# A graph layer on one core: norm split in two, gate ahead of it, three more picks, and smaller moves in setup and tail

## The chip, the cores and the metric

The kernel runs on one core of a Trainium2 chip. Its engines are TensorE (PE; its weight loads are listed as PEld), VectorE (DVE), ScalarE (ACT), GpSimd (POOL) and SyncE (SP), which only issues DMAs. The metric is the device time of one execution in microseconds; the time before is the median of three runs. Every engine works through its own queue in the order of the program; the program's order is written out by hand here (`tc.manual_schedule()`), so where a line stands decides when its engine comes to it.

## What is computed

200,000 edges, sorted by destination, between 6,250 nodes of 64 features:

```python
w = silu(edge_attr @ W1 + b1) @ W2 + b2                          # (E, 9)
msg = einsum('ef,em,fmg->eg', x[src], edge_sh * w, W_tp)         # (E, 64)
agg = segment_sum(msg, dst, N) / sqrt(AVG_DEG)                   # AVG_DEG = 16
gamma, beta = split(silu(node_vec[:, None] @ Wn1 + bn1) @ Wn2 + bn2)
out = layernorm(x + agg * (1 + gamma) + beta)                    # each row of 64
```

## The kernel before

**Tiles.** 128 edges make a tile, 16 tiles a block; there are 1,563 tiles and 98 blocks, the last one of 11 tiles. Nodes are in 49 blocks of 128.

**Rows of x.** A tile's 128 source rows come in one of three ways. Most tiles are gathered from HBM by POOL, one indirect DMA per tile (`gather`, L99), six blocks ahead (`AHEAD`); nothing else is on POOL's queue in the main loop. In 23 blocks (`SPG`, every fourth from 7) the first tile comes as 128 single-row DMAs from SP (`load_rows`, L115), 32 of them in each of four iterations. And the last three or four tiles of each block are *picked* out of SBUF by TensorE: `hots` (L521, VectorE) makes one-hot matrices from the tile's keys, `pick` (L536) multiplies them with x in 14 matmuls of 448 columns, one for each of seven column groups and for the high and the low part of x, and VectorE masks and reduces the result (`xm` L545, `hs` L547). `picked(g)` says how many tiles of block g are picked: four, and three where g is divisible by six, which makes 375 picks and 1,165 gathers.

**Keys.** A key tells in which partition and column of x in SBUF a source row lies. Keys are worked out on VectorE for many blocks at once, turned by TensorE (`keys_turn`, L177), copied by ScalarE to `kt` and stored by SP to a table `kd` in HBM (L179), from which `load_keys` (L453) broadcasts them two blocks at a time. Three such tables are stored: one in setup, one each for iterations 3 and 5, whose stores wait in the list `stores` until the next iteration begins.

**One iteration i** of the main loop works on several blocks. It first issues `gather(i + 6)`, then SP's work: whatever is in `stores`; on even i `load(i + 2)`, the edge attributes `ea` (L433, 512 KB for two blocks) and `sh` (L435); on odd i `load_keys`; then `load_rows`. TensorE's order is:

- pick 0 of block i+1, with the matmuls of `nodes(i)` between its own;
- `hidden(i + 2)` (L465), which needs `ea`, and on ScalarE its Silu (L474);
- `second(i + 1)` (L483), which needs PSUM bank "s";
- `windows(i)` (L569), which needs all rows of block i;
- on odd i `project` (L616), with W_tp, for two blocks;
- picks 1, 2 and 3 of block i+1. `weights(i + 1)` on VectorE goes with pick 1.

**Nodes.** `nodes(i)` holds one bank "s" tile `ps`. Into it go the product for the gate of node block i-2 (L661), the placing of sums by node (`place`, L632), and, in every fourth iteration from 7 to 95, the finished sums of two node blocks (`bring`, L648). `gate` (L405, L406) reads its product from `ps` into `gam` and `xb`; it runs for 49 node blocks, up to iteration 50. `bring` calls `finish`, and this `finish_nodes`, the norm: on VectorE `y` = sums x gam (L770), + xb (L771), mean (L773, L774), subtract (L775), square (L777), sum (L779); Sqrt on ScalarE (L782); reciprocal (L783) and the output `o` (L785) on VectorE. All of it stands in VectorE's queue where `bring` is, ahead of the gate. The store of `o` (L418) goes into `stores`.

**Banks.** PSUM tiles are by tag: "px" and "pz" with two buffers, "p1" (two banks: hidden layer, and the transposed projection `pt`), "s" and "r" with one. The keys of a block, `pk` (L515), are in "r", and so is the projection `pr` (L610) of the first block, which has no partner.

**Setup** splits x into a high part (`xs[0]`, L277, ScalarE) and a rest (`xs[1]`, L278, VectorE), in seven pieces; it reads x in order and writes with a stride of seven elements, the layout that the picks need.

**Tail.** After the last pick come the matmuls of the last two node blocks into one tile `py_n` (L739, L743), the windows of block 97, its projection `pr_n` (L751) in 10 matmuls, its placing (L754), and one norm over both node blocks.

Of the kernel before, what the change touches and what calls it, by code (L numbers as in the profile page):

```python
# [7 lines left out]
F32 = mybir.dt.float32  # L8
# [16 lines left out]
KW = KB * W  # L25
ZT = 8
FB = 2
AHEAD = 6
LB = 2
# [21 lines left out]

def picked(g):

    return Q - (g % 6 == 0)


def tiles(g):
# [10 lines left out]
def gnn_resnorm_kernel(ctx: ExitStack, tc: tile.TileContext, x, src, dst, dst_row, ea, sh, cn,  # L68
# [18 lines left out]
    with ExitStack() as fast:  # L87
# [85 lines left out]
        def keys_turn(g0, kf, tag, kt):  # L173

            c0 = g0 * Q
            p_kt = psum.tile([P, P], F32, tag=tag, name=f"p_kt{g0}", bufs=1 + (tag == "pz"))
            nc.tensor.transpose(p_kt, kf, ident)  # L177
            nc.scalar.copy(kt, p_kt)
            stores.append(lambda: nc.sync.dma_start(kd[c0:c0 + P, :], kt))  # L179

        def relative(k0, k1):
            nc.vector.tensor_sub(rel[:, k0:k1], dst_i[:, k0:k1], row_r[:, k0:k1])
# [9 lines left out]
        def setup(temp):  # L192
# [79 lines left out]
                return spread  # L272

            def split(h):
                xh = gam[:, h * J:(h + 1) * J, :]
                hi, lo_ = [xs[i][:, h].rearrange("p f l -> p l f") for i in range(2)]
                nc.scalar.copy(hi, xh)  # L277
                nc.vector.tensor_sub(lo_, xh, hi.bitcast(F32))  # L278

            kb = [ztw[:, k * LB * Q:(k + 1) * LB * Q] for k in range(6)]  # L280
            for f in keys_of(0, LB, kb):
# [29 lines left out]
            pick(0, 2)  # L311
            hidden(1, act=False)
            kt = temp.tile([P, P], F16)
            keys_turn(LB, kb[0], "pz", kt)
            hidden_act(1)
            while stores:
                stores.pop(0)()
            load_keys(LB)
            p_row = psum.tile([len(SPG), P], F32, tag="pz", name="p_row", bufs=2)
            nc.tensor.transpose(p_row, row_f, ident)  # L320
# [88 lines left out]

        stores = []  # L410

        def finish(j0, j1, sums, parts=None):
            y = late.tile([P, j1 - j0, F], F32, tag="y", name=f"y{j0}")
            end = finish_nodes(nc, late, eps, sums, y, gam[:, j0:j1, :], xb[:, j0:j1, :], j0)

            def store():
                o = end()
                stores.append(lambda: nc.sync.dma_start(out_v[:, j0:j1, :], o))  # L418

            if parts is None:  # L420
                store()
            else:
                parts.append(store)


        ea_t, sh_t, oh_t, kr_t, st, a, zs = {}, {}, {}, {}, {}, {}, {}
# [175 lines left out]
        def project(q):  # L602


            gs = pair(q)
            z = [zs.pop(g).rearrange("p c k w -> p c (k w)") for g in gs]
            if len(gs) == 1:
                pr = psum.tile([P, 1, F], F32, tag="r", name=f"pr{q}")
                for c in range(5):
                    nc.tensor.matmul(pr[0:KW, 0], z[0][:, c], wtc2[:, c, :], start=(c == 0), stop=(c == 4))  # L610
                halves(q, pr[0:KW])
# [12 lines left out]

            return [lambda: None, lambda: None, turn]
# [16 lines left out]

            return [lambda k=k: part(k) for k in range(len(gs))]

        def bring(j0, j1, py, ends=None):

            def part(j):
                nc.tensor.matmul(py[:, j - j0], yt.pop(j), ident2, start=True, stop=True)  # L648
                if j == j1 - 1:
                    finish(j0, j1, py[:, 0:j1 - j0], ends)  # L650

            return [lambda j=j: part(j) for j in range(j0, j1)]

        def nodes(i):


            ps = psum.tile([P, 4, P], F32, tag="s", name=f"ps{i}")
            parts = []
            if 0 <= i - 2 < NJ:
                def product(j=i - 2):  # L660
                    nc.tensor.matmul(ps[:, 2], ht[j // 4 % 2][:, j % 4], wn2a, start=True, stop=True)  # L661
                parts.append(product)
            if i % 2 == 0 and i >= 2:
                parts += place(i // 2 - 1, ps[:, 0:2].rearrange("p a n -> p (a n)"))
            j = (i - 5) // 2
            if i % 2 == 1 and i >= 5 and j % FB == FB - 1:
                parts += bring(j + 1 - FB, j + 1, ps[:, 3].rearrange("p (j f) -> p j f", f=F))
            if 0 <= i - 2 < NJ:
                parts.append(lambda: gate(i - 2, ps[:, 2]))
            if i == 60:  # L670
                parts.append(lambda: reach_all(ps[0:1, 3, 0:4]))
            return parts

        with tc.manual_schedule(), tc.tile_pool(name="temp", bufs=1) as temp:
# [2 lines left out]
                       6: [lambda k=k: relative(KN + k, min(KN + k + 352, NBLK * KB))  # L677
                           for k in range(0, NBLK * KB - KN, 352)]}

            for i in range(1, NBLK):  # L680
                if i + AHEAD < NBLK:
                    gather(i + AHEAD)
# [46 lines left out]
            ends = []  # L729
            for f in bring(q - 2, q - 1, psum.tile([P, 1, F], F32, tag="r", name="py_l"), ends):  # L730
                f()
            windows(g - 1)
            sums(g)
            pick(g, 2, [ends])
            pick(g, 3, [project(q)])
            while stores:
                stores.pop(0)()
            py = psum.tile([P, FB, F], F32, tag="s", name="py_n")
            nc.tensor.matmul(py[:, 0], carry.pop(q - 1), ident2, start=True, stop=False)  # L739
            for b in range(2):  # L740
                for k, h in enumerate(pair(q)):
                    for s in range(2):
                        nc.tensor.matmul(py[:, b], hot[h][:, b * P:(b + 1) * P], r[q][:, k, s],  # L743
                                         start=(b == 1 and k == 0 and s == 0), stop=(b == 0 and k == 1 and s == 1))
# [4 lines left out]
            pr = psum.tile([P, F], F32, tag="r", name="pr_n")  # L749
# [6 lines left out]
            while stores:  # L756
                stores.pop(0)()


    bad_n = nc.values_load(flag_i[0:1, 0:1], min_val=0, max_val=4 * P,  # L760
# [6 lines left out]
def finish_nodes(nc, work, eps, sums, y, gam, xb, tag):  # L767

    n = y.shape[1]
    nc.vector.tensor_mul(y, sums, gam)  # L770
    nc.vector.tensor_add(y, y, xb)  # L771
    mean = work.tile([P, n], F32, tag="mean", name=f"mean{tag}")
    nc.vector.tensor_reduce(mean, y, AX.X, ALU.add)  # L773
    nc.vector.tensor_scalar(mean, mean, 1.0 / F, None, op0=ALU.mult)  # L774
    nc.vector.tensor_sub(y, y, mean.unsqueeze(2).to_broadcast([P, n, F]))  # L775
    sq = work.tile([P, n, F], F32, tag="sq", name=f"sq{tag}")
    nc.vector.tensor_mul(sq, y, y)  # L777
    var = work.tile([P, n], F32, tag="var", name=f"var{tag}")
    nc.vector.tensor_reduce(var, sq, AX.X, ALU.add)  # L779

    def end():
        nc.scalar.activation(var, var, AF.Sqrt, bias=eps, scale=1.0 / F)  # L782
        nc.vector.reciprocal(var, var)  # L783
        o = work.tile([P, n, F], F32, tag="o", name=f"o{tag}")
        nc.vector.tensor_mul(o, y, var.unsqueeze(2).to_broadcast([P, n, F]))  # L785
        return o

    return end


def general_path(tc, dram, x, dst_row, ea, sh, src_i, dst_i, w1bd, b1c, w2bd, b2r, wtc,
# [3 lines left out]
    with ExitStack() as ctx:  # L795
# [109 lines left out]
        for j0 in range(0, NJ, JC):  # L905
# [7 lines left out]
            o = finish_nodes(nc, work, eps, a[0], a[0], gam[:, js, :], xb[:, js, :], f"g{j0}")()  # L913
            nc.sync.dma_start(out_v[:, js, :], o)


# [47 lines left out]
```

## Time and profile before

| | us |
|---|---|
| median of three runs (1487.76 to 1489.39) | 1488.75 |
| profiled execution, its own time | 1488.34 |
| profiled execution, span | 1486.5 |
| PE busy in the span | 1443.6 (97%) |
| DVE busy | 1210.6 (81%) |
| POOL busy | 1108.5 (75%) |
| ACT busy | 515.7 (35%) |

The span runs from the first to the last instruction of the profiled execution. A busy share is an average over stages. In the profile, "L99" is line 99 of the kernel; "out<-in" gives the tiles written and read by the program's names with their numbers left out; "x" is a count. A row of the costliest groups ends with the engine's idle time just before its instructions and with what ended most of it ("issue" means that the profile shows nothing that the engine waited for). A row of the waits has a waiting engine and line, what released it, the total in us, how often, and the longest.

### The profile page before, as it was taken

How to read it: one execution, taken by the hardware profiler on the slowest of the kernel's cores; microseconds unless marked ns; L12 is line 12 of the kernel's file. 1: busy time of each engine (PE TensorE's matmuls, PEld its weight loads, DVE VectorE, ACT ScalarE, POOL GpSimd, SP SyncE). 2: the span in 40 equal slices, each digit the busy share in tenths (PEclk: the TensorE clock that was granted, in tenths of full speed). 3: DMA queues.
4: the chain of work that ended last, by engine and by line, in shares of the span. 5: the costliest groups of instructions: out<-in, count | busy, mean ns of one | idle time of the engine just before them, and what ended most of it. 6: DMA issues, size and time to landing. Idle time of an engine off the chain costs nothing.

```text
span 1486.5 us, 34308 instructions
## 1 busy us (share of the span) xinstructions
PE 1443.6 (97%) x10905; PEld 1211.5 (82%) x10905; DVE 1210.6 (81%) x2188; ACT 515.7 (35%) x1324; POOL 1108.5 (75%) x1174
## 2 busy tenths in 40 slices
PE   7899999999999999999999999999999999999997
PEld 5687888888888888888878888888888888888886
DVE  8788887887878888888797888888887888888875
ACT  4324333242433333424243324233242333333332
POOL 7777777777777777777777777777777777777773
PEclk9999999999999999999999999999999999999998
DMA  6422222222223222222232222222222222232310
GB/s 194 96 50 61 73 60 64 68 63 64 55 57 74 62 61 55 77 56 63 55 72 55 61 65 63 61 56 63 64 62 54 73 55 61 55 74 61 73 29 19
DMA packets 90168, 96.03 MB, mean 65 GB/s; under 512 B 36696, under 2 KB 51242, under 8 KB 89978
## 3 DMA queue, kind: packets, MB, share of 16 engines
q0 software_dynamic: 37280, 38.25, 13.4%
q1 hardware_dynamic: 52122, 53.89, 12.5%
q8 instruction: 89, 1.46, 0.4%
q10 hardware_dynamic: 576, 1.61, 0.3%
q14 instruction: 101, 0.83, 0.2%
HBM read 91.91 MB, written 1.73 MB: 63 GB/s over the span
## 4 chain that ended last, share of the span: by engine, by line
PE 79%; POOL 5%; DVE 5%; issue 4%; DMA 3%; ACT 3%; SPq 2%; ACTq 0%; DVEq 0%; POOLq 0%
PE px L536 60%; PE pz L569 6%; POOL hs L99 5%; PE p L465 5%; PE pt L616 3%; PE p L483 3%; DMA hs<-in_x_dram,src_i 2%; SPq L115 1%; ACT st L474 1%; DVE xm L545 1%; ACT L474 1%; PE ps L632 1%; DVE hs L547 1%; PE ps L661 1%; DVE hot_k L521 0%
## 5 line engine op out<-in xcount | busy, mean ns | idle before, releaser
L99 POOL DMA_INDIRECT hs<-in_x_dram,src_i x1165 | 1107.2, 950 | 357.1 <-issue 321.1
L536 PE MATMUL px<-xs_w,hot_k 128*128 128x448 f32 x5250 | 1125.2, 368 | 1.5 <-DVE hot_k L521 1.4
L536 PEld LDWEIGHTS px<-xs_w,hot_k 128*128 128x128 f32 x5250 | 961.2, 189 | 79.9 <-DVE xm L545 2.3
L545 DVE SCALAR_TENSOR_TENSOR xm<-li,jl,px 128x448 f32<-128x448 f32 x375 | 253.4, 676 | 205.3 <-PE px L536 202.6
L521 DVE TENSOR_TENSOR hot_k<-pk,nk 128x896 fp32r<-128x896 f32 x375 | 390.9, 1081 | 0.6 <-ACT pk L515 0.6
L547 DVE TENSOR_REDUCE hs<-xm 128x64 f32<-128x448 f32 x375 | 232.5, 620 | 12.9
L474 ACT ACTIVATE st<-p,b1c 128x1024 f32<-128x1024 f32 x98 | 109.2, 1114 | 374.8 <-PE p L465 374.5
L580 ACT COPY ztw<-pz 64x140 f32<-64x140 f32 (+1 forms) x780 | 208.6, 267 | 14.1 <-PE pz__24815 L569 3.0
L569 PEld LDWEIGHTS pz<-a,hs 128*64 128x64 f32 x3116 | 99.6, 138 | 44.2 <-issue 39.3
L503 DVE TENSOR_TENSOR a<-oh,p 128x1008 f32<-128x1008 f32 x98 | 117.9, 1204 | 3.3
L638 ACT COPY carry<-ps 128x128 f32<-128x128 f32 x48 | 12.7, 265 | 304.8 <-PE ps L632 304.8
L569 PE MATMUL pz<-a,hs 128*64 128x63 f32 x3116 | 112.8, 225 | 4.4 <-DMA hs<-in_x_dram,src_i 1.6
L465 PE MATMUL p<-ea,w1bd 64*128 64x512 f32 x392 | 110.7, 641 | 2.3 <-DMA ea<-in_ea_dram 2.3
L483 PEld LDWEIGHTS p<-st,w2p 128*32 128x32 f32 x784 | 15.8, 108 | 80.7 <-issue 38.5
L782 ACT ACTIVATE var<-var,eps 128x2 f32<-128x2 f32 (+1 forms) x25 | 7.4, 295 | 202.0 <-DVE var L779 202.0
L483 PE MATMUL p<-st,w2p 128*32 128x256 f32 x784 | 62.6, 391 | 7.6 <-DVE xb L406 7.6
L616 PE MATMUL pt<-ztw,wtc 128*64 128x112 f32 x960 | 55.3, 261 | 3.1 <-ACT st L474 2.5
L515 ACT CAST pk<-kr 128x512 f32<-128x512 f16 (+1 forms) x96 | 54.9, 572 | 7.2 <-issue 7.2
L465 PEld LDWEIGHTS p<-ea,w1bd 64*128 64x128 f32 x392 | 29.6, 185 | 31.5 <-issue 24.4
L497 DVE TENSOR_TENSOR p<-p,sh 128x72 f32<-128x72 f32 x196 | 47.3, 241 | 6.7
L616 PEld LDWEIGHTS pt<-ztw,wtc 128*64 128x64 f32 x960 | 46.8, 137 | 5.0 <-ACT st L474 3.9
L486 ACT ACTIVATE p2s<-p,b2c 128x256 f32<-128x256 f32 x98 | 45.7, 466 | 5.7 <-PE p L483 5.7
(150 smaller groups left out, 503.3 us busy)
## 6 DMA issues: line engine op xcount, KB each, us to landing
hs<-in_x_dram SPq DMA_DIRECT2D x2944, 0.2 KB
ea<-in_ea_dram SPq DMA_DIRECT2D x48, 512.0 KB
hs<-in_x_dram,src_i POOLq DMA_INDIRECT x1165
kr<-kd SPq DMA_DIRECT2D x48, 256.0 KB
sh<-in_sh_dram SPq DMA_DIRECT2D x49, 144.0 KB
cb<-cn_d SPq DMA_DIRECT2D x12, 128.0 KB
out_dram<-o SPq DMA_DIRECT2D x24, 64.0 KB
dst_i<-in_dst_dram SPq DMA_DIRECT2D x1, 768.0 KB
```

The source lines that it names most:

```text
L99: hs_dma[g] = [nc.gpsimd.indirect_dma_start(out=hs[g][:, t - g * KB, :], out_offset=None, in_=x, in_offset=bass.IndirectOffsetOnAxis(ap=sr ...
L465: nc.tensor.matmul(p1[:, i, :].rearrange("p (c t e) -> p c t e", c=4, t=4), w1bd[i * 64:(i + 1) * 64, :], e[i * 64:(i + 1) * 64, :].rearra ...
L474: nc.scalar.activation(st[g], p1_t.pop(g), AF.Silu, bias=b1c)
L483: nc.tensor.matmul(p2[g][c * D:(c + 1) * D, 0, :].rearrange("p (i e) -> p i e", i=2), w2p, s[:, :, c * P:(c + 1) * P], start=True, stop=True)
L503: nc.vector.tensor_mul(a[g], oh_t.pop(g)[:, :, None, :].to_broadcast([P, KB, M, W]), sw.unsqueeze(3).to_broadcast([P, KB, M, W]))
L521: nc.vector.tensor_tensor(hot_k[g, t], pk_t[g][:, t, None, :].to_broadcast([P, J, P]), nk.unsqueeze(2).to_broadcast([P, J, P]), op=ALU.is_ ...
L536: nc.tensor.matmul(px.rearrange("p f l -> p (f l)"), hot_k[g, t][:, h, :], xs[i][:, h].rearrange("p f l -> p (f l)"), start=(h == 0 and i ...
L545: nc.vector.scalar_tensor_tensor(xm, li[:, None, :].to_broadcast([P, F, J]), jl[:, c:c + 1], px, op0=ALU.is_equal, op1=ALU.mult)
L547: nc.vector.tensor_reduce(hs[g][:, tiles(g) - q + t, :], xm, AX.X, ALU.add)
L569: mm = nc.tensor.matmul(pz[v][v * F:(v + 1) * F, k // 2].rearrange("p m w -> p (m w)"), hsg[:, k0 + k, :], ag[:, k0 + k].rearrange("p m w ...
L580: copy(z[h * F:(h + 1) * F, 0:5 - h, k0 + v:k0 + n:2, :].rearrange("p m k w -> p k m w"), pz[v][v * F:(v + 1) * F, 0:(n + 1 - v) // 2, h:M ...
L616: nc.tensor.matmul(pt[h * F:(h + 1) * F, 0, 0:KW], wtc2[:, c, :], z[h][:, c], start=(c == 0), stop=(c == 4))
```

## The change

- `picked`: three picks where g is divisible by seven instead of six, hence 378 picks and 1,162 gathers.
- `nodes`: the gate comes ahead of the norm. `bring` holds its matmuls alone; `finish` follows the gate.
- `finish_nodes` is cut into three: the product with gam at once; a `middle` (from the addition to the Sqrt) that the loop calls after pick 1 of the next block; an `end` (reciprocal, output, and the store put into `stores`) that it calls after pick 2.
- Key tables of iterations 3 and 5: their stores wait in a list of their own, `tables`, which is emptied behind the loads and row copies of the next iteration.
- `project` of group 0 takes tag "p1" instead of "r".
- `split` reads x with the stride and writes in order.
- Tail: the first windows of block 97 go ahead of the matmuls of the last node blocks; these two have a bank each; the last projection goes in two halves of its output rows; each of the two is normed alone by `finish_block`, with the bn_stats and bn_aggr instructions.

```diff
 def picked(g):
-    return Q - (g % 6 == 0)
+    return Q - (g % 7 == 0)
...
             def split(h):
-                xh = gam[:, h * J:(h + 1) * J, :]
-                hi, lo_ = [xs[i][:, h].rearrange("p f l -> p l f") for i in range(2)]
-                nc.scalar.copy(hi, xh)
-                nc.vector.tensor_sub(lo_, xh, hi.bitcast(F32))
+                xh = gam[:, h * J:(h + 1) * J, :].rearrange("p l f -> p f l")
+                nc.scalar.copy(xs[0][:, h], xh)
+                nc.vector.tensor_sub(xs[1][:, h], xh, xs[0][:, h].bitcast(F32))
...
-        def finish(j0, j1, sums, parts=None):
+        def finish(j0, j1, sums):
             y = late.tile([P, j1 - j0, F], F32, tag="y", name=f"y{j0}")
-            end = finish_nodes(nc, late, eps, sums, y, gam[:, j0:j1, :], xb[:, j0:j1, :], j0)
+            middle, end = finish_nodes(nc, late, eps, sums, y, gam[:, j0:j1, :], xb[:, j0:j1, :], j0)
             def store():
                 o = end()
                 stores.append(lambda: nc.sync.dma_start(out_v[:, j0:j1, :], o))
...
+            ends.extend([middle, store])
+
+        def finish_block(j, sums):
+            y = late.tile([P, 1, F], F32, tag="y", name=f"y{j}")[:, 0]
+            nc.vector.tensor_mul(y, sums, gam[:, j])
+            nc.vector.tensor_add(y, y, xb[:, j])
+            st = late.tile([P, 6], F32, tag="sq", name=f"st{j}")
+            nc.vector.bn_stats(st, y)
+            mv = late.tile([P, 2], F32, tag="mean", name=f"mv{j}")
+            nc.vector.bn_aggr(mv, st)
+            var = late.tile([P, 1], F32, tag="var", name=f"var{j}")
+            nc.scalar.activation(var, mv[:, 1:2], AF.Sqrt, bias=eps)
+            def end():
+                nc.vector.reciprocal(var, var)
+                o = late.tile([P, 1, F], F32, tag="o", name=f"o{j}")
+                nc.vector.tensor_scalar(o[:, 0], y, mv[:, 0:1], var, op0=ALU.subtract, op1=ALU.mult)
+                nc.sync.dma_start(out_v[:, j:j + 1, :], o)
+            return end
...
             if len(gs) == 1:
-                pr = psum.tile([P, 1, F], F32, tag="r", name=f"pr{q}")
+                pr = psum.tile([P, 2, 4 * P], F32, tag="p1", name=f"pr{q}")
...
         def nodes(i):
...
+            whole = i % 2 == 1 and i >= 5 and j % FB == FB - 1
+            if whole:
+                parts += bring(j + 1 - FB, j + 1, py)
             if 0 <= i - 2 < NJ:
                 parts.append(lambda: gate(i - 2, ps[:, 2]))
+            if whole:
+                parts.append(lambda: finish(j + 1 - FB, j + 1, py))
...
             for i in range(1, NBLK):
                 if i + AHEAD < NBLK:
                     gather(i + AHEAD)
                 while stores:
                     stores.pop(0)()
...
+                while tables:
+                    tables.pop()()
...
                 pick(i + 1, 1, [weights(i + 1), turn])
+                if ends:
+                    ends.pop(0)()
...
                     if t < Q:
                         pick(i + 1, t)
+                    if t == 2 and ends:
+                        ends.pop(0)()
                 if i in (3, 5):
-                    keys_turn(LB + KC * (i - 1) // 2, kb[0], "s", kt)
+                    tables.append(keys_turn(LB + KC * (i - 1) // 2, kb[0], "s", kt))
...
-            py = psum.tile([P, FB, F], F32, tag="s", name="py_n")
-            nc.tensor.matmul(py[:, 0], carry.pop(q - 1), ident2, start=True, stop=False)
+            windows(g, [0])
+            py = [psum.tile([P, F], F32, tag=tag, name=f"py_{tag}") for tag in ("s", "r")]
+            nc.tensor.matmul(py[0], carry.pop(q - 1), ident2, start=True, stop=False)
...
-            windows(g, [0])
             marks(NJ)
             windows(g, [ZT])
...
             for c in range(5):
-                nc.tensor.matmul(pr[0:KW], z[:, c], wtc2[:, c, :], start=(c == 0), stop=(c == 4))
+                for k0, k1 in ((0, F), (F, KW)):
+                    nc.tensor.matmul(pr[k0:k1, 0, 0:F], z[:, c, k0:k1], wtc2[:, c, :], start=(c == 0), stop=(c == 4))
+            end = finish_block(q - 1, py[0])
             last = work.tile([KW, F], F32, tag="rt", name="last")
-            nc.vector.tensor_copy(last, pr[0:KW])
-            nc.tensor.matmul(py[:, 1], hot[g][:, 0:P].bitcast(F32), last, start=False, stop=True)
-            finish(q - 1, NJ, py)
-            while stores:
-                stores.pop(0)()
+            nc.vector.tensor_copy(last, pr[0:KW, 0, 0:F])
+            end()
+            nc.tensor.matmul(py[1], hot[g][:, 0:P].bitcast(F32), last, start=False, stop=True)
+            finish_block(q, py[1])()
...
 def finish_nodes(nc, work, eps, sums, y, gam, xb, tag):
     n = y.shape[1]
     nc.vector.tensor_mul(y, sums, gam)
-    nc.vector.tensor_add(y, y, xb)
...
+    def middle():
+        nc.vector.tensor_add(y, y, xb)
...
+        nc.vector.tensor_reduce(var, sq, AX.X, ALU.add)
+        nc.scalar.activation(var, var, AF.Sqrt, bias=eps, scale=1.0 / F)
     def end():
-        nc.scalar.activation(var, var, AF.Sqrt, bias=eps, scale=1.0 / F)
         nc.vector.reciprocal(var, var)
         o = work.tile([P, n, F], F32, tag="o", name=f"o{tag}")
         nc.vector.tensor_mul(o, y, var.unsqueeze(2).to_broadcast([P, n, F]))
         return o
-    return end
+    return middle, end
```

More of the change, by code (lines that the diff above doesn't have):

```diff
@@ L178, in keys_turn @@
             nc.scalar.copy(kt, p_kt)
-            stores.append(lambda: nc.sync.dma_start(kd[c0:c0 + P, :], kt))
+            return lambda: nc.sync.dma_start(kd[c0:c0 + P, :], kt)
         def relative(k0, k1):
@@ L313, in setup @@
             kt = temp.tile([P, P], F16)
-            keys_turn(LB, kb[0], "pz", kt)
+            keys_turn(LB, kb[0], "pz", kt)()
             hidden_act(1)
-            while stores:
-                stores.pop(0)()
             load_keys(LB)
@@ L410, in gnn_resnorm_kernel @@
         stores = []
-        def finish(j0, j1, sums, parts=None):
+        ends = []
+        def finish(j0, j1, sums):
             y = late.tile([P, j1 - j0, F], F32, tag="y", name=f"y{j0}")
-            end = finish_nodes(nc, late, eps, sums, y, gam[:, j0:j1, :], xb[:, j0:j1, :], j0)
+            middle, end = finish_nodes(nc, late, eps, sums, y, gam[:, j0:j1, :], xb[:, j0:j1, :], j0)
             def store():
@@ L418, in store @@
                 stores.append(lambda: nc.sync.dma_start(out_v[:, j0:j1, :], o))
[L420 to L423, printed above, removed]
+            ends.extend([middle, store])
[15 more added lines that the diff above has]
+            return end
         ea_t, sh_t, oh_t, kr_t, st, a, zs = {}, {}, {}, {}, {}, {}, {}
@@ L607, in project @@
             if len(gs) == 1:
-                pr = psum.tile([P, 1, F], F32, tag="r", name=f"pr{q}")
+                pr = psum.tile([P, 2, 4 * P], F32, tag="p1", name=f"pr{q}")
                 for c in range(5):
-                    nc.tensor.matmul(pr[0:KW, 0], z[0][:, c], wtc2[:, c, :], start=(c == 0), stop=(c == 4))
-                halves(q, pr[0:KW])
+                    nc.tensor.matmul(pr[0:KW, 0, 0:F], z[0][:, c], wtc2[:, c, :], start=(c == 0), stop=(c == 4))
+                halves(q, pr[0:KW, 0:1, 0:F])
                 return []
@@ L643, in place, with bring @@
             return [lambda k=k: part(k) for k in range(len(gs))]
[L645 to L652, printed above, removed]
+        def bring(j0, j1, py):
+            return [lambda j=j: nc.tensor.matmul(py[:, j - j0], yt.pop(j), ident2, start=True, stop=True)
+                    for j in range(j0, j1)]
         def nodes(i):
@@ L665, in nodes @@
             j = (i - 5) // 2
-            if i % 2 == 1 and i >= 5 and j % FB == FB - 1:
-                parts += bring(j + 1 - FB, j + 1, ps[:, 3].rearrange("p (j f) -> p j f", f=F))
+            py = ps[:, 3].rearrange("p (j f) -> p j f", f=F)
+            whole = i % 2 == 1 and i >= 5 and j % FB == FB - 1
+            if whole:
+                parts += bring(j + 1 - FB, j + 1, py)
             if 0 <= i - 2 < NJ:
                 parts.append(lambda: gate(i - 2, ps[:, 2]))
+            if whole:
+                parts.append(lambda: finish(j + 1 - FB, j + 1, py))
             if i == 60:
@@ L678, in gnn_resnorm_kernel @@
                            for k in range(0, NBLK * KB - KN, 352)]}
+            tables = []
             for i in range(1, NBLK):
@@ L728, in gnn_resnorm_kernel @@
             pick(g, 1, [weights(g)])
-            ends = []
-            for f in bring(q - 2, q - 1, psum.tile([P, 1, F], F32, tag="r", name="py_l"), ends):
-                f()
+            py = psum.tile([P, 1, F], F32, tag="r", name="py_l")
+            for f in bring(q - 2, q - 1, py):
+                f()
+            finish(q - 2, q - 1, py)
+            ends.pop(0)()
             windows(g - 1)
@@ L742, in gnn_resnorm_kernel @@
                     for s in range(2):
-                        nc.tensor.matmul(py[:, b], hot[h][:, b * P:(b + 1) * P], r[q][:, k, s],
+                        nc.tensor.matmul(py[b], hot[h][:, b * P:(b + 1) * P], r[q][:, k, s],
                                          start=(b == 1 and k == 0 and s == 0), stop=(b == 0 and k == 1 and s == 1))
-            windows(g, [0])
             marks(NJ)
@@ L748, in gnn_resnorm_kernel @@
             z = zs.pop(g).rearrange("p c k w -> p c (k w)")
-            pr = psum.tile([P, F], F32, tag="r", name="pr_n")
+            pr = psum.tile([P, 2, 4 * P], F32, tag="p1", name="pr_n")
             for c in range(5):
-                nc.tensor.matmul(pr[0:KW], z[:, c], wtc2[:, c, :], start=(c == 0), stop=(c == 4))
+                for k0, k1 in ((0, F), (F, KW)):
+                    nc.tensor.matmul(pr[k0:k1, 0, 0:F], z[:, c, k0:k1], wtc2[:, c, :], start=(c == 0), stop=(c == 4))
+            end = finish_block(q - 1, py[0])
             last = work.tile([KW, F], F32, tag="rt", name="last")
-            nc.vector.tensor_copy(last, pr[0:KW])
-            nc.tensor.matmul(py[:, 1], hot[g][:, 0:P].bitcast(F32), last, start=False, stop=True)
-            finish(q - 1, NJ, py)
-            while stores:
-                stores.pop(0)()
+            nc.vector.tensor_copy(last, pr[0:KW, 0, 0:F])
+            end()
+            nc.tensor.matmul(py[1], hot[g][:, 0:P].bitcast(F32), last, start=False, stop=True)
+            finish_block(q, py[1])()
     bad_n = nc.values_load(flag_i[0:1, 0:1], min_val=0, max_val=4 * P,
@@ L770, in finish_nodes @@
     nc.vector.tensor_mul(y, sums, gam)
-    nc.vector.tensor_add(y, y, xb)
[L772 to L777, printed above, removed]
-    var = work.tile([P, n], F32, tag="var", name=f"var{tag}")
-    nc.vector.tensor_reduce(var, sq, AX.X, ALU.add)
+    var = work.tile([P, n], F32, tag="var", name=f"var{tag}")
+    def middle():
+        nc.vector.tensor_add(y, y, xb)
+        mean = work.tile([P, n], F32, tag="mean", name=f"mean{tag}")
+        nc.vector.tensor_reduce(mean, y, AX.X, ALU.add)
+        nc.vector.tensor_scalar(mean, mean, 1.0 / F, None, op0=ALU.mult)
+        nc.vector.tensor_sub(y, y, mean.unsqueeze(2).to_broadcast([P, n, F]))
+        sq = work.tile([P, n, F], F32, tag="sq", name=f"sq{tag}")
+        nc.vector.tensor_mul(sq, y, y)
+        nc.vector.tensor_reduce(var, sq, AX.X, ALU.add)
+        nc.scalar.activation(var, var, AF.Sqrt, bias=eps, scale=1.0 / F)
     def end():
-        nc.scalar.activation(var, var, AF.Sqrt, bias=eps, scale=1.0 / F)
         nc.vector.reciprocal(var, var)
@@ L912, in general_path @@
             nc.vector.tensor_add(a[0], a[0], a[2])
-            o = finish_nodes(nc, work, eps, a[0], a[0], gam[:, js, :], xb[:, js, :], f"g{j0}")()
-            nc.sync.dma_start(out_v[:, js, :], o)
+            middle, end = finish_nodes(nc, work, eps, a[0], a[0], gam[:, js, :], xb[:, js, :], f"g{j0}")
+            middle()
+            nc.sync.dma_start(out_v[:, js, :], end())
 _INS = ['x', 'src', 'dst', 'dst_row', 'ea', 'sh', 'cn', 'w1', 'b1', 'w2', 'b2', 'wtp',
```

## The prediction

> **What bounds it now.** I read the page's busy shares, its costliest groups, the waits, a table by stage, then the timelines of one stage.
>
> ```profile
> PE 1443.6 (97%) x10905; PEld 1211.5 (82%) x10905; DVE 1210.6 (81%) x2188; ACT 515.7 (35%) x1324; POOL 1108.5 (75%) x1174
> ...
> L99 POOL DMA_INDIRECT hs<-in_x_dram,src_i x1165 | 1107.2, 950 | 357.1 <-issue 321.1
> L536 PE MATMUL px<-xs_w,hot_k 128*128 128x448 f32 x5250 | 1125.2, 368 | 1.5 <-DVE hot_k L521 1.4
> ```
>
> TensorE is busy 97% of the span, 78% of that in the picks (375 x 14 matmuls). POOL looks freer than it is: its 357 us of idle time is almost all "issue", 0.3 us between gathers, so a gather costs 1.25 us and the 1165 of them run without a break from 4.0 to 1466.2. So there are two streams, and TensorE's is the longer one: the windows matmuls (L569) of the last block start at 1472.07, 5.9 us after its last gather.
>
> The stage table cuts the span at the hidden-layer matmuls (L465) of successive blocks, taken as a block's zero time h:
>
> ```profile
> 667.28:682.09 14.81, 14.81 (x107) 12.59 (x106) 11.78 (x22) 5.28 (x12) 11.32 (x12) 1.00 0.23 55
> 682.09:699.02 16.93, 15.99 (x127) 13.31 (x126) 14.66 (x30) 6.41 (x16) 12.75 (x14) 1.00 0.31 71
> 699.02:713.38 14.36, 14.36 (x104) 12.14 (x103) 12.00 (x20) 3.99 (x11) 10.90 (x12) 1.00 0.25 48
> 713.38:729.06 15.68, 15.68 (x127) 13.32 (x126) 12.08 (x23) 5.33 (x15) 11.83 (x13) 1.00 0.36 89
> ```
>
> Columns: stage, its length, then busy time of PE, PEld, DVE, ACT and POOL. The second and fourth do the same TensorE work (127 matmuls), but the second follows a norm of two node blocks and takes 1.25 us more, with PE idle for 0.94. The waits say whom it waits for:
>
> ```profile
> PE p L483 <- DVE xb L406: 7.6, 11, 0.7
> ```
>
> Eleven times the gate (L406) stands on VectorE behind the whole norm, and second() waits for the bank that the gate reads. Over all stages the excess after a norm is 12.8 us for the eleven norms up to iteration 47 (with a gate) and 6.2 for the twelve later ones (0.5 each): 19.0.
>
> The SP queue decides the forecast. The norm's store heads it, and the next edge load stands behind:
>
> ```profile
> 683.53 0.41 SPq L418 DMA_DIRECT2D out_dram<-o  x1
> 683.98 0.47 SPq L433 DMA_DIRECT2D ea<-in_ea_dram  x1
> ```
>
> VectorE's o ended at 683.50: the store leaves 0.03 us after it, the load 0.45 later. The waits of SP put 108.8 us on this store (L418 on o, L785). Today the load still comes 15 us ahead of its use at 699.02. What happens when it doesn't stands in the chain of waits for the key table's store of iteration 4, the same order in the queue:
>
> ```profile
> 96.16 3.72 DMA ea<-in_ea_dram
> 99.88 0.47 issue
> 100.35 0.69 PE p L465
> ```
>
> kt was ready at 95.71, TensorE got going at 100.35: 4.6 us, of which it stood 1.8.
>
> **The skill.** "DMA: Bandwidth & Descriptors" (Anatomy of one DMA) says that "any semaphore wait happens on the issuing sequencer before dispatch", as SP shows, and fits 2.0 us + bytes/436e3 (for GpSimd's path): an estimate of 3.2 us for these 512 KB. The packets here end 3.0 to 3.3 us after the issue with no store ahead, 3.4 to 4.0 (median 3.75) right behind one. "TensorE: Matmul & The Clock Gate" (Part 1) has the clock halved after an idle window of some 3.4 us: the trace has 0.5 from 50.96 for 6.8 us, after TensorE stopped at 48.2. "ScalarE: Activation LUTs" (What ACT_TABLE_LOAD costs) gives 1283 ns, as measured here, plus a drain that this trace does not show. "SBUF — State Buffer" (the note on 16-byte cachelines) charges every access that crosses to a new line, as a 28-byte stride does; no row here tells reads from writes.
>
> **The change, part by part** (us against the profiled execution: span 1486.5, time 1488.34, 0.41 under the median of the runs).
>
> *Picks.* 14 instead of 17 blocks pick three times: 3 more picks. A stage with three is 2.80 shorter (12.88 against 15.68): +8.4. POOL loses 3 gathers, 3.75, on a stream that isn't the longer one.
>
> *Norm split, gate ahead.* Before TensorE's next wait only the product with gam (0.3) stays; the other work moves behind picks 1 and 2. Stages without a norm show what is left: -19.0. ScalarE now swaps tables to Sqrt and back (1.28 each) in the second half of an iteration and at its end, where it idles for 7 us or more: nothing.
>
> But o is later. In the stage from 713.38, pick 1's xm starts at h+6.9 and pick 2's could start at h+9.7. New order: xm and reduce (1.25) to h+8.2; six norm operations (0.33+0.32+0.20+0.33+0.33+0.29) to h+10.0; xm and reduce to h+11.3; reciprocal and o (0.2+0.3) to h+11.8. The next hidden matmuls would start at h+15.68 (15.46 once the gates are over, o then at 11.65), so 3.9 to 3.8 remain. Store and load need 0.03+0.45+3.75+0.40 (packets' end to matmul, 0.38 and 0.42 in the two waits seen) = 4.63. TensorE, in order, stands 0.75; bounds 0.3 and 1.1 from 3.4 and 4.0. Queued behind that hidden layer are the next second, windows and picks, all of TensorE; on SP, behind the store, the other loads and row copies, which have a block or more to spare; POOL's queue holds only gathers, which wait for none of this. This is new: the store was never late enough. There are 22 norms with a load behind (iterations 7 to 91). At three of them the next block (28, 56, 84) has three picks, so only 1.05 remains: 3.55 each. 19 x 0.75 + 3 x 3.55 = +25.
>
> *Clock.* After each of those three long stands the clock may halve for a window or two; half a window is 1.7. A wait of 1.8 at 100 us halved nothing, one of 5.8 did. I take +2, bounds 0 and 6.
>
> *Group 0's projection in p1.* It stood 5.80 until the keys of block 3 had been read in its old bank (53.93). Now it waits for ztw's copies (to 52.0) only: -1.9, and 0.8 less at half clock: -2.7, bounds -1.5 and -4.
>
> *Key table stores behind the loads.* Both loads concerned are in time: the 1.8, and 1.24 at the second (a stage of 14.12 against 12.88): -3.1. The tables are read 27 iterations later at the earliest. Setup's own table store keeps its place on SP.
>
> *Split.* Seven copies of 0.88 and seven subtractions of 0.91, the size of which contiguous would be about 0.50 (hot_k, twice as large, takes 1.00). If only writes pay, 2.8 of VectorE time go; TensorE, at half clock there with 1.17 per step, gives back 0.3. If strided reads cost more, 1.5 is lost: -0.3, bounds -1 and +1.5.
>
> *Tail.* First windows ahead of nine py matmuls (1.13): ztw's copies start earlier, -1.0 (0 to -1.1). Last projection in two column halves: 2.14 for 10 matmuls at half clock; pt's 20 in halves take 1.11, -0.85 (0 to -1.5). Norm of one block: the chain from 1477.52 to 1480.51 becomes seven operations of 0.2 to 0.3 (from py_l's rows), 1.73, -1.25; bn_stats and bn_aggr have no row, taken as the reductions they resemble (0.25, 0.2; 0 and 0.6 together as bounds). Sum -3.1. Block 47's norm hides beside the projection.
>
> **Sum.** -19.0 + 8.4 + 25.0 + 2.0 - 2.7 - 3.1 - 0.3 - 3.1 = +7.2: span 1493.7, and on the median 1488.75 + 7.2 = **1496.0**.
>
> **Rivals.** 0.2% (3.0 us) is about what a measurement of this kernel can tell from no change.
>
> *The load is in time; POOL bounds (faster).* If store and load need 3.9 or less, the 19 waits are nothing, the three are about 3, and TensorE alone would gain 10. But gathers set a floor: block 93's end at 1412.41, less 2.5 for two fewer, plus 1.4 to land: windows at 1411.3 instead of 1417.42. From there one more pick (+2.8) and no norm wait (-0.45) leave the last pick 3.8 earlier; with the tail -6.9: 1481.9. For it: loads with no store ahead land in 3.0 to 3.3, and the second key table's wait took 4.0. Against: the 22 loads behind a store. The sum crosses zero at 0.37 per norm, a need of 4.2.
>
> *About even.* A need of 4.2: waits of 0.37 x 19: 1488.8.
>
> *Slower still.* Landing at 4.0 (1.0 x 19, three of 3.8) and a halved clock after all three (+6): 1503. For it: the load meets the gathers' packets; against: 1.8 us of idle time did no harm.
>
> *A part does not do what it says*: the split gains nothing or loses 1.5; alone it cannot turn the sign.
>
> **Numbers.** Forecast 0.50, its own range 1490.5 to 1501.5; POOL-bound 0.20; even 0.16; slower still 0.14. The range for 8 in 10 runs from the POOL floor, 1481.5, to 1502. Faster 0.20 and 0.03 of the even case: 0.23; same 0.10 of it and 0.03 of the forecast: 0.13; slower 0.64.
>
> **What would show it.** Right: stages after a norm back at 15.7 and 15.5; no wait of L483 on L406; in their place L465 waiting for the DMA of ea, some 22 times, three of them over 3 us, with the store of o leaving about 11.8 after h; L610 idle near 3.9; POOL's last gather near 1462.4, with L569 never waiting for it. Wrong: L465 not waiting, or L569 waiting for hs from about block 65 on, which is the POOL case; VectorE late with xm of pick 2; half clock in mid-run.

## The result, and the profile after

| | before | after |
|---|---|---|
| median, six runs each, us | 1488.53 | 1495.35 (1493.0 to 1497.58) |
| ratio to before, 95% interval | | 1.0042 (1.0029 to 1.0056) |
| span of the profiled execution | 1486.5 | 1494.6 |

The changed kernel is slower by 6.8 us; the prediction had 7.2; how much of that was luck is told below. In its profile the lines have moved: the hidden layer is L481 (L465 before), second L499, the picks L552, xm L561, windows L585, `pt` L632, the store of `o` L417, `o` L813, the load of `ea` L449. (The kernels e6, e7 and e8 below ran only in sets in which the kernel before itself took 2390 to 2411 us instead of 1489, so their ratios hold within those sets alone.)

Of the page, the busy shares and three of the costliest groups:

```profile
PE 1454.7 (97%) x10957; PEld 1219.7 (82%) x10957; DVE 1215.5 (81%) x2200; ACT 513.2 (34%) x1323; POOL 1103.7 (74%) x1171
...
L99 POOL DMA_INDIRECT hs<-in_x_dram,src_i x1162 | 1102.4, 949 | 356.0 <-issue 316.8
L552 PE MATMUL px<-xs_w,hot_k 128*128 128x448 f32 x5292 | 1136.0, 369 | 2.1 <-DVE hot_k L537 1.4
...
L481 PE MATMUL p<-ea,w1bd 64*128 64x512 f32 x392 | 111.6, 646 | 18.3 <-DMA ea<-in_ea_dram 17.9
```

TensorE is as busy as before, 42 more picks' matmuls included. What is new is the last row: the hidden layer has 18 us of idle time ahead of it, and a DMA ended 17.9 of it. The waits of all engines name it twice, once for the weight loads and once for the matmuls:

```profile
PEld p L481 <- DMA ea<-in_ea_dram: 28.0, 27, 3.9
PE p L481 <- DMA ea<-in_ea_dram: 17.9, 21, 3.5
```

The wait for the gate (7.6 us, 11 times, at L483 in the kernel before) is gone; in its place TensorE waits for the edge attributes, up to 3.5 us. The chain of waits around one of them, the load for block 46:

```profile
691.47 0.30 DVE o L813
691.77 0.02 issue
691.78 0.41 SPq L417
692.20 0.04 issue
692.24 3.64 DMA ea<-in_ea_dram
695.88 0.04 issue
695.92 1.12 PE p L481 x3
```

Read downwards, it is the prediction's chain link by link: `o` ends, the store leaves, the load leaves 0.46 later, and 3.7 after that TensorE starts. Over the 22 norms `o` ends 11.6 (median) after its stage's start, where 11.8 and 11.65 were worked out, and TensorE starts 4.25 (median) after `o`; 4.63 were expected, and 3.8 to 3.9 would have cost nothing.

The table by stage (length, then busy time of PE, PEld, DVE, ACT, POOL, the granted clock, and the DMA's share and GB/s), two ordinary stages around a norm and then a short block behind one:

```profile
665.11:679.93 14.82, 14.82 (x107) 12.59 (x107) 11.77 (x21) 3.99 (x11) 11.17 (x13) 1.00 0.20 56
679.93:695.92 15.99, 15.75 (x126) 13.31 (x125) 14.54 (x32) 7.64 (x17) 12.03 (x14) 1.00 0.25 72
...
858.73:874.39 15.66, 12.73 (x110) 10.46 (x109) 14.93 (x31) 7.63 (x17) 11.84 (x13) 1.00 0.28 73
874.39:889.99 15.60, 15.60 (x101) 12.93 (x101) 10.65 (x15) 4.13 (x11) 11.79 (x13) 0.89 0.19 47
```

The stage after a norm has gone from 16.93 to 15.99, 0.3 above one without a norm. The stage from 858.73 belongs to a block with three picks: 12.73 of work in 15.66, so TensorE stands for 2.93. The stage after it shows the second bill: no idle time, but a mean clock of 0.89 and 15.60 in place of 14.11. The clock is at half from 875.4 for 3.41 us; the same follows the other two short blocks, at 455.6 and 1291.8.

Where the 8.1 us of the two spans come from, by stages:

| | predicted | in the two profiles |
|---|---|---|
| norm: old excess gone, new waits for ea | -19.0 + 25.0 | -19.7 + 19.8 (19 x 0.52, 3 x 3.34) |
| three more picks | +8.4 | +8.4 |
| half clock after three long waits | +2.0 | +4.5 (3 x 1.5) |
| setup up to block 4's hidden layer (bank, split) | -3.0 | -2.9 |
| key table stores | -3.1 | -2.4 |
| tail, without its one more pick | -3.1 | -2.3 |
| four loads of ea further on in SP's queue | | +1.1 |
| six stages with slower picks | | +1.9 |
| one stage that was longer in the kernel before | | -0.3 |

Two rows need a word. One of the 19 stages, 0.86 longer, has no wait for `ea`; e1 has the same 0.86 there. And the late store holds up more than the load right behind it. Here is SP's queue from the store ahead of block 14's load on, with two batches of row copies between this load and the next:

```profile
212.00 0.42 SPq L417 DMA_DIRECT2D out_dram<-o  x1
212.47 0.46 SPq L449 DMA_DIRECT2D ea<-in_ea_dram  x1
...
215.68 10.79 SPq L115 DMA_DIRECT2D hs<-in_x_dram  x32
...
229.48 10.29 SPq L115 DMA_DIRECT2D hs<-in_x_dram  x32
239.82 0.41 SPq L449 DMA_DIRECT2D ea<-in_ea_dram  x1
```

TensorE needed that next load at 243.45 and stood until 243.80. Four such waits, 0.09 to 0.35 us, account for most of the 1.1; the prediction had given these loads a block or more to spare. In the six other stages the picks' matmuls start 207 ns apart instead of 200; why is open.

### The profile page after: what moved, and what is told of

It reads as the page before. It is cut to its first block, busy times and chain, and to the rows that moved or that the text cites. A ratio compares the mean times of both kernels' runs of the same rounds, so it can differ in the third digit from the quotient of the medians.

```text
span 1494.6 us, 34421 instructions
## 1 busy us (share of the span) xinstructions
PE 1454.7 (97%) x10957; PEld 1219.7 (82%) x10957; DVE 1215.5 (81%) x2200; ACT 513.2 (34%) x1323; POOL 1103.7 (74%) x1171
## 3 DMA queue, kind: packets, MB, share of 16 engines
q0 software_dynamic: 37184, 38.15, 11.6%
HBM read 91.81 MB, written 1.73 MB: 63 GB/s over the span
## 4 chain that ended last, share of the span: by engine, by line
PE 65%; DVE 13%; DMA 9%; POOL 7%; issue 4%; SPq 2%; ACT 0%; DVEq 0%; POOLq 0%; ACTq 0%
PE px L552 48%; POOL hs L99 7%; DMA ea<-in_ea_dram 6%; PE p L481 5%; PE pz L585 5%; PE p L499 3%; DMA hs<-in_x_dram,src_i 3%; DVE xm L561 3%; DVE hot_k L537 2%; PE pt L632 2%; DVE hs L563 2%; SPq L115 1%; DVE a L519 1%; SPq L417 1%; DVE c L616 1%
## 5 line engine op out<-in xcount | busy, mean ns | idle before, releaser
L552 PE MATMUL px<-xs_w,hot_k 128*128 128x448 f32 x5292 | 1136.0, 369 | 2.1 <-DVE hot_k L537 1.4
L552 PEld LDWEIGHTS px<-xs_w,hot_k 128*128 128x128 f32 x5292 | 970.3, 188 | 83.0 <-issue 2.3
L561 DVE SCALAR_TENSOR_TENSOR xm<-li,jl,px 128x448 f32<-128x448 f32 x378 | 255.5, 676 | 210.2 <-PE px L552 207.4
L490 ACT ACTIVATE st<-p,b1c 128x1024 f32<-128x1024 f32 x98 | 109.1, 1114 | 595.2 <-PE p L481 595.2
L585 PEld LDWEIGHTS pz<-a,hs 128*64 128x64 f32 x3116 | 100.9, 139 | 42.2 <-issue 39.4
L481 PE MATMUL p<-ea,w1bd 64*128 64x512 f32 x392 | 111.6, 646 | 18.3 <-DMA ea<-in_ea_dram 17.9
L585 PE MATMUL pz<-a,hs 128*64 128x63 f32 x3116 | 114.7, 227 | 1.3 <-ACT ztw L596 1.3
L499 PEld LDWEIGHTS p<-st,w2p 128*32 128x32 f32 x784 | 15.5, 108 | 73.4 <-issue 49.9
L481 PEld LDWEIGHTS p<-ea,w1bd 64*128 64x128 f32 x392 | 29.7, 186 | 49.4 <-DMA ea<-in_ea_dram 28.0
L499 PE MATMUL p<-st,w2p 128*32 128x256 f32 x784 | 64.3, 400 | 0.0
L632 PE MATMUL pt<-ztw,wtc 128*64 128x112 f32 x960 | 54.8, 260 | 0.9 <-ACT ztw L596 0.9
L509 DVE STREAM_TRANSPOSE p<-p2s 128x256 f32<-128x256 f32 x98 | 44.1, 450 | 4.7 <-ACT p2s L502 4.7
L632 PEld LDWEIGHTS pt<-ztw,wtc 128*64 128x64 f32 x960 | 46.8, 137 | 1.4 <-ACT ztw L596 1.1
```

Of the source, the lines that this page charges most:

```text
L481: nc.tensor.matmul(p1[:, i, :].rearrange("p (c t e) -> p c t e", c=4, t=4), w1bd[i * 64:(i + 1) * 64, :], e[i * 64:(i + 1) * 64, :].rearra ...
L490: nc.scalar.activation(st[g], p1_t.pop(g), AF.Silu, bias=b1c)
L499: nc.tensor.matmul(p2[g][c * D:(c + 1) * D, 0, :].rearrange("p (i e) -> p i e", i=2), w2p, s[:, :, c * P:(c + 1) * P], start=True, stop=True)
L552: nc.tensor.matmul(px.rearrange("p f l -> p (f l)"), hot_k[g, t][:, h, :], xs[i][:, h].rearrange("p f l -> p (f l)"), start=(h == 0 and i ...
L561: nc.vector.scalar_tensor_tensor(xm, li[:, None, :].to_broadcast([P, F, J]), jl[:, c:c + 1], px, op0=ALU.is_equal, op1=ALU.mult)
L585: mm = nc.tensor.matmul(pz[v][v * F:(v + 1) * F, k // 2].rearrange("p m w -> p (m w)"), hsg[:, k0 + k, :], ag[:, k0 + k].rearrange("p m w ...
```

## The experiments

Theory A is the prediction's: the load of `ea`, held on SP behind the store of `o`, makes TensorE wait. Its rivals here: B, that the norm's middle on VectorE holds pick 2; C, that the three picks cost everything and the norm's move is neutral.

### e1: the output stores behind the loads

```diff
                 if i + AHEAD < NBLK:
                     gather(i + AHEAD)
-                while stores:
-                    stores.pop(0)()
...
+                while stores:
+                    stores.pop(0)()
                 while tables:
                     tables.pop()()
```

> The changed kernel with one difference: the list of output stores is emptied behind the loads and row copies of the iteration, beside the key tables, instead of ahead of them. Theory A (the load of ea, held on SP behind the store of o, is what TensorE waits for): the waits of L481 for ea go, 19 of about 0.5 and 3 of about 3.3 us (19.8), and the three halvings of the clock with them (4.5). TensorE alone would then end near 1471, so the gathers become the bound: 1480 to 1482, with L585 waiting for hs from about block 65 on. Theory B (the norm's middle part on VectorE, between picks 1 and 2, holds the pick): no change, 1495. Theory C (the three picks more cost everything, the norm split is neutral): no change, 1495.

Measured: 1482.11, ratio to before 0.9957 (0.9944 to 0.9971). One pair of lines moved on one queue turns 6.8 us lost into 6.6 won; B and C foresaw no change, and the norm's middle stands where it stood. The wait of L481 for `ea` is gone from the list of waits, and 19 of the 22 stages behind a norm last as long as one without; in the kernel before none did. Another wait has come:

```profile
PE pz L585 <- DMA hs<-in_x_dram,src_i: 6.5, 3, 2.6
```

That is the floor set by POOL, in the timeline of TensorE at block 84:

```profile
1275.98 0.64 PE L499 MATMUL p<-st,w2p 128*32 128x256 f32 x8
1278.64 1.06 PE L585 MATMUL pz<-a,hs 128*64 128x63 f32 x29 [2.02 <-DMA hs<-in_x_dram,src_i]
```

POOL finished block 84's last gather at 1276.26, 2.4 us before. Without a norm's wait TensorE catches up with gathers that run without a break, to 1462.3. The halved clock did not go altogether: two of the new waits, of 2.35 and 2.55 us, are each followed by 3.41 us of it. Around the second, with the columns of the table by stage:

```profile
1067.00:1071.26 4.26, 1.71 (x13) 0.49 (x13) 4.23 (x6) 1.48 (x2) 3.33 (x4) 1.00 0.43 90
1071.26:1076.00 4.74, 4.74 (x42) 4.26 (x43) 1.96 (x4) 2.63 (x9) 3.54 (x4) 0.64 0.14 32
```

So the rival of the prediction called "POOL bounds", 1481.9, was the right picture of this kernel, and not of the changed one.

### e2: the three short blocks moved by one

```diff
-    return Q - (g % 7 == 0)
+    return Q - (g == 0 or (g % 7 == 0 and g % 28 != 0) or (g > 1 and g % 28 == 1))
```

> The changed kernel with the three blocks of three picks that follow a norm (28, 56, 84) replaced by their neighbours 29, 57, 85; still 378 picks. Theory A: the three waits of 3.0 to 3.6 us shrink to about 0.5 each (-8.5) and the three stretches at half clock go (-4.5): 1482.4, TensorE just above the gathers' floor of about 1480; the 22 small waits for ea stay. Theory B: a norm's middle is the same in any block, no change, 1495. Theory C: no change, 1495.

Measured: 1482.88, ratio 0.9961 (0.9952 to 0.9969). With the same 378 picks, and all 22 norms as in the changed kernel, 12.5 us go by keeping short blocks away from norms; B and C, with no change, are wrong here too. Its waits:

```profile
PE p L481 <- DMA ea<-in_ea_dram: 13.1, 25, 1.6
```

The longest is 1.6 instead of 3.5, and the clock is at full speed from 55 us to the tail.

### e3: 375 picks as before

```diff
-    return Q - (g % 7 == 0)
+    return Q - (g % 6 == 0)
```

> The changed kernel with picked(g) of before (three picks where g is divisible by six, 375 picks). Theory A: three picks less are -8.4, but seven short blocks follow a norm with a load behind it (12, 24, ... 84) instead of three: 4 more waits of 3.3 in place of 0.5 (+11.3) and 4 more stretches at half clock (+5.9), sum +8.8: 1504. Theory C: 8.4 faster, 1487, as without the other parts. Theory B: 1487, since the norm's middle takes the same time with either number.

Measured: 1504.64, ratio 1.0116 (1.0092 to 1.0139). Fewer picks make it 9.3 slower, since seven short blocks follow a norm (stage excess 2.9 to 3.5 each, 22.3 in all) and the clock halves after four of these seven waits, twice for 6.83 us instead of 3.41. B and C, which foresaw 1487, are wrong a third time.

```profile
PE p L481 <- DMA ea<-in_ea_dram: 26.9, 22, 3.4
```

### e4: the norm in one piece, behind the gate

```diff
-                parts.append(lambda: finish(j + 1 - FB, j + 1, py))
+                parts.append(lambda: (finish(j + 1 - FB, j + 1, py), ends.pop(0)(), ends.pop(0)()))
```

> The changed kernel with the norm of the main loop in one piece again, but still behind the gate: middle and end are called right after finish. Theory A: o is early, so no wait for ea (-19.8) and no half clock (-4.5); but VectorE's one-hot matrices start some 2.5 us later after a norm, as in the late stages of the kernel before, where no gate was held and 0.5 was lost: 23 x 0.5 = +11.5. Sum -12.8: 1482.6. If putting the gate ahead gains nothing, the 19.7 of before are back: 1490.8. Theory B: -19.8 for the holds in the middle and about the same 11.5 back, so the time cannot tell A from B; the stages can, since under B VectorE's xm of pick 2 is late in the changed kernel. Theory C: 1495.

Measured: 1488.02, ratio 0.9995 (0.9987 to 1.0004). There are no waits for `ea`, as A has it, but I missed by 5.4: the stage after a norm loses 1.1 in most cases with a gate and 0.5 to 0.7 without, 20.6 in all, about as in the kernel before (19.7). Taking the gate from behind the norm, alone, has gained nothing. Of the 20.6, 18.1 are lost before pick 1 begins. The waits show what took its place:

```profile
PE pt L632 <- ACT st L490: 13.5, 23, 1.6
```

From the timeline of ScalarE and TensorE after one norm:

```profile
681.00 0.29 ACT L808 ACTIVATE var<-var,eps 128x2 f32<-128x2 f32 x1 [9.11 <-DVE var L807]
681.31 1.28 ACT L490 ACT_TABLE_LOAD   x1
...
682.61 1.11 ACT L490 ACTIVATE st<-p,b1c 128x1024 f32<-128x1024 f32 x1
...
683.77 1.18 PE L632 MATMUL pt<-ztw,wtc 128*64 128x112 f32 x20 [0.85 <-ACT st L490]
```

Sqrt is followed by the load of Silu's table; only then does `st` read the hidden layer out of bank "p1", and `pt`, which has the same bank, waits for that.

### e5: the same without a table swap

In this kernel the square root of the main loop's norms is left out.

```diff
-        nc.scalar.activation(var, var, AF.Sqrt, bias=eps, scale=1.0 / F)
+        nc.scalar.activation(var, var, AF.Identity, bias=eps, scale=1.0 / F)
```

> The kernel with the norm in one piece behind the gate, with one difference: the square root of the main loop's norms is left out (Identity in place of Sqrt on ScalarE, of the same size), so ScalarE never swaps its table there. That kernel took 1488.0 and lost 1.1 per norm with a gate and 0.5 per later norm (20.6 in all). Theory D (that loss is ScalarE's: the Silu table comes back 1.28 us late, the hidden layer's Silu starts late, ztw's copies after it, and the projection waits): the loss falls to some 2, TensorE alone would end near 1469 and the gathers bound it: 1480 to 1482. Theory E (the loss is VectorE's, whose one-hot matrices start 2.9 us late): no change, 1488.

Measured: 1485.33, ratio 0.998 (0.997 to 0.999). The tables are loaded 3 times instead of 49, `st` starts 0.05 after its matmuls in all but two of the stages after a norm (1.1 in e4's, median), and `pt` no longer waits for it. Yet the stages after a norm still lose 17.5 of the 20.6. In the waits:

```profile
PE px L552 <- DVE xm L561: 10.2, 19, 1.0
```

Now TensorE waits at the start of pick 3 for a buffer that VectorE, late by the norm, has not read yet: 15.9 of the 17.5 are lost there, where e4 lost 1.6. So theory D is wrong by its own number (1480 to 1482). E named the right engine, but its "no change" is 2.7 off as well. Three waits of about the same length lie side by side after a norm: the gate, the table with bank "p1", and VectorE's backlog. Taking away one shows the next; moving the work away, as the split does, takes away all three, as e1's stages show.

### e6, e7 and e8: not settled

- e6, 382 picks on top of e1 (`g % 10`), ratio 0.9917 (0.9893 to 0.9941):

> The kernel with the output stores behind the loads (1482.1 with 378 picks), with 382 picks (three picks where g is divisible by ten). If the gathers bound that kernel (POOL): four gathers less lower their floor by 5, while TensorE alone goes from about 1471 to 1471 + 4 x 2.80 = 1482; so about the same time, 1480 to 1483. If TensorE bounds it: 1482.1 + 11.2 = 1493.

- e7, the kernel before with group 0's projection in "p1" and the key tables' stores behind the loads alone, ratio 0.9991 (0.9967 to 1.0015):

> The kernel before with two of the small parts alone: group 0's projection in p1, and the key tables' stores behind the loads. By the sum of the prediction -2.7 - 3.1: 1482.9. If these waits are hidden behind others later on, less: 1488. The gathers, which end 5.9 us ahead of the last windows, allow about 4.4 of it before they bound: so at least 1484 if the prediction's floor is right.

- e8, 381 picks on top of e1 (`g % 9`) and in the tail `ends.pop(0)()` behind `windows(g - 1)`, ratios 0.9911 (0.9882 to 0.994), 0.9962 (0.9936 to 0.9988) and 0.9934 (0.9896 to 0.9972) in three sets:

> A version meant to beat both: output stores behind the loads, 381 picks (three where g is divisible by nine), and in the tail the norm's middle behind the windows of block 96, so that ScalarE's Sqrt no longer stands ahead of ztw's copies (1.3 us of TensorE's wait in the changed kernel). Gathers: floor 1480 - 3.75; TensorE alone: 1471 + 8.4 - 1.3 = 1478. Both near 1478 to 1480; if waits for gathers of up to 2.5 us remain, 1481. A kernel with the stores behind the loads that TensorE bounded at 1482 would take 1482 + 8.4 - 1.3 = 1489 here.

In all of these, and in two earlier runs of e5 (ratios 0.9886 and 0.9946), VectorE stands for some 1000 us in all ahead of `xm`, most of it ended by what the view calls "remote", a release that the profile does not trace to an instruction of the kernel. e6's page:

```profile
L561 DVE SCALAR_TENSOR_TENSOR xm<-li,jl,px 128x448 f32<-128x448 f32 x382 | 258.5, 677 | 996.4 <-remote 777.2
```

With such waits neither POOL nor the loads bound anything, so these ratios say nothing of the causes told here. That POOL bounds e1 stands on e1's own waits; whether more picks would better it is open, and so is the time of e7's parts alone. Of e1 to e4, e1 and e2 beat both kernels clearly; joining the two was not tried.

## Why the prediction was right, and where it was off

- **The mechanism was right.** o's end, the queue on SP, the wait of L481 and its place are as worked out. e1 and e2 show it from both sides, and e3 follows the same sum (1504 expected, 1504.64 measured, nearer than its own scatter of 1501.6 to 1507.7).
- **The number was right by luck.** With the waits for `ea` as they came out, 19.8 instead of 25.0, the prediction's own sum is +2.0 and not +7.2; too little half clock (2.5), the later loads and slower picks (3.0), tables and tail (1.5) made up for it. Its borders between the cases were off too: by its own terms the sum crosses zero at a small wait of 0.43, a need of 4.28, not 0.37 and 4.2, and the need measured is 4.25. 1503 for the slowest rival comes to 1505 by its terms.
- **"Landing at 3.75" was too long.** It was taken from loads behind a store in the kernel before. In the changed kernel the packets end 3.34 us after the issue (median), with 4.25 from `o` to the matmul in place of 4.63. The stages behind a norm came out 0.52 longer instead of 0.75, the three short ones 3.34 instead of 3.55: 5.2 less in all. Why the packets are faster was not tested.
- **"Half clock: +2"** was too low: all three long waits were followed by one stretch of 3.41 us at half clock, 1.5 us each. As the Trainium skill's page "TensorE: Matmul & The Clock Gate" (Part 1) has it, the window is some 3.4 us; but a stand of 2.93 was enough here, less than the idle window that it names, and 2.35 was in e1, while stands of 2.92 and 3.28 in e3 halved nothing. What tells them apart in these traces stands in the last section.
- **"Norm split, gate ahead: -19.0"** was right as a sum (-19.7) and wrong in its reason. I read the wait of L483 on the gate as what an early norm costs. e4 took it away and gained nothing; the split gains because it also moves VectorE's work and the Sqrt. A wait in the profile names the last of several; that the others are shorter doesn't follow.
- **Tail: -3.1 against -2.3.** I overlooked that the tail's norm of block 46 now sends Sqrt to ScalarE ahead of `ztw`'s copies. ScalarE's timeline:

```profile
1475.61 0.29 ACT L808 ACTIVATE var<-var,eps 128x1 f32<-128x1 f32 x1 [5.33 <-DVE var L807]
1475.81 2.20 ACT L596 COPY ztw<-pz 64x140 f32<-64x140 f32 x8
```

  Counted from the windows that they copy, the copies start 2.4 us later than in the kernel before, and `pt` takes 2.39 instead of 1.11. The last projection gains more than worked out, 2.13 to 0.80 in place of 0.85 less; part of that is the clock, which halves at 1486.39 here, behind it, and at 1474.31, just ahead of it, in the kernel before. The single norm (2.99 to 1.84 from its first operation to `o`) came out as worked out: bn_stats takes 0.23 and bn_aggr 0.18.
- **Group 0's bank, split, key tables** came out near their sizes, which says little of the first two: the five other kernels at 1482 to 1505 with this setup reach block 4's hidden layer 2.6 to 5.4 us before the kernel before does, with half-clock stretches in other places or, in e1, none. The projection starts at 51.94 instead of 53.95 and the picks after it at 52.95 instead of 55.80. But it stands 1.43, not 3.9, and not for `ztw`'s copies: its line ends with `[1.43 <-ACT st L490]`, the Silu that reads bank "p1" until 51.89. That both readings give 52 is chance. The split's subtractions take 0.90 per piece (0.91 before) and its copies 0.92 (0.88): reading with the stride costs as much as writing with it.

## What to carry to other kernels

When work is moved to a later place, follow what it produces to the next queue: a store that waits at the head of a queue holds every load behind it, and the price is paid by the engine that needs those loads. Put stores behind the loads of the same iteration, and ask at which blocks the slack is smallest; three blocks of 98 cost here 8.5 us more than three ordinary ones behind a norm, as much as all three added picks, and 13 with their half clock. When a wait is removed, look for the ones beside it before booking its length as a gain.

## What the runs showed of the hardware

*The clock.* TensorE's clock halved for 3.41 us, or twice that, and each 3.41 us cost about 1.5. How long TensorE stands doesn't decide alone: nine stands of 2.35 to 3.53 us in the main loops were followed by half clock (three in the changed kernel, two in e1, four in e3), two of 2.92 and 3.28 us in e3 were not, nor were the shorter ones, up to 2.02. But the stretches start whole multiples of 3.413 us apart: in the changed kernel 123 of them lie between 455.57 and 875.41, and 122 between that and 1291.83. Cut at these points, each of the nine intervals just ahead of a halving has 2.2 us or more without a matmul, and no other interval of a main loop, in the seven kernels that took 1482 to 1505, has more than 1.73. The two stands of e3 each lay across such a point. In setup this limit doesn't hold (1.3 was enough ahead of 35.73 in the changed kernel), and why two stretches in e3 are twice as long is open.

*Queues and engines.* A store that waited for its data at the head of SP's queue held the load behind it, which left 0.46 us after the store. Loading Silu's table takes 1.28 us, and the next activation starts 0.01 to 0.02 later, with no further delay. VectorE and ScalarE take the same time, within 5%, for 448 elements read with a stride of 28 bytes as for those written with it.
